# Third and fourth block of a cross-attention kernel: a new order of residual loads, stores, moves, row sums, scores and statistics

## The chip, the cores and the metric

The kernel runs on one core of one Trainium2 chip. The metric is the device time of one execution in microseconds (us). Before the change the median of three runs is 1057.76 us (1057.69 to 1058.13).

The core's engines are named as the profile names them: PE is TensorE's matmul, PEld its weight load, DVE is VectorE, ACT ScalarE, POOL GpSimd, and SP SyncE, which here only issues transfers (DMAs). L949 is line 949 of the kernel before.

## The reference

Sixteen batches of 1024 rows x 512 features are updated by cross-attention to 64 context rows each, with 16 heads of 32 features. Both inputs of the attention are layer-normalised and then scaled and shifted by a per-batch vector.

```python
def _ada_ln(x, c, W_ss, b_ss):
    mu = jnp.mean(x, axis=-1, keepdims=True)
    var = jnp.mean((x - mu) ** 2, axis=-1, keepdims=True)
    h = (x - mu) / jnp.sqrt(var + EPS)
    ss = jax.nn.silu(c) @ W_ss + b_ss
    scale, bias = jnp.split(ss, 2, axis=-1)
    return (1.0 + scale)[:, None, :] * h + bias[:, None, :]
...
xq = _ada_ln(x_q, t_vec, Wss_q, bss_q)
xkv = _ada_ln(x_kv, t_vec, Wss_kv, bss_kv)
q = (xq @ Wq + bq).reshape(B, Lq, nh, dh)
kv = (xkv @ Wkv + bkv).reshape(B, Lkv, 2, nh, dh)
...
scores = jnp.einsum('bqhd,bkhd->bhqk', q, k) / jnp.sqrt(jnp.float32(dh))
attn = jax.nn.softmax(scores, axis=-1)
out = jnp.einsum('bhqk,bkhd->bqhd', attn, v).reshape(B, Lq, H)
return x_q + (out @ Wp + bp)
```

All data are float32.

## The kernel before

The rows are cut into 32 blocks of 512 (two to a batch), numbered 0 to 31. A block passes through these stages; the small functions that do them are called one by one in an order written out by hand: one list of calls for the start (L972 to L1191), a loop over blocks 4 to 29 (L1194 to L1288), and a list for the end. Nothing reorders the calls: each engine runs its instructions in the order in which the calls issue them, and so does SP with its transfers. Waits between engines are put in from the data dependences. In the built program SP's transfers use eight semaphores in turn, so that a transfer is also not issued before the one eight places ahead of it has landed.

The stages of a block i, with their engines and lines:

- `load_x(i)` (SP, L143) loads the block, 1 MB. It needs a free buffer of two, which `turn` of block i-2 gives up. `q_stats(i)` (DVE, L263/L264) takes mean and variance of its 512 rows, in four tiles of 128. `q_scale(i)` computes the inverse root: five small ACT instructions (L279 to L284), then, for blocks above 2, four small POOL instructions (L285 to L288). This is "the root". `hidden(i)` (ACT, L324) normalises in place.
- `turn(i)` (DVE, L503) and `move(i)` (16 small transfers, L516) together transpose the block into `xt`. Block 5 splits the 16 transfers between SP and POOL, block 4 and those from 6 on have all on SP. `scale_features(i)` (ACT, L573) applies scale and shift.
- `feature_sums(i)` (POOL, L608 to L611) and seven `query_product(i, n)` (PE, L633) form the queries with one product fewer than eight, in two PSUM banks, 0 and 1. `query_seed` (ACT, L645) and `query_out` (ACT, L663) copy from them, `query_added` (DVE, L670) adds. Query products 1, 6, 5 and 3 accumulate in bank 0 one after another, so a product has to wait until the copy or add of the one before has read the bank.
- `scores(i, z)` (PE, L681; z is 0 or 1, half of the context rows) writes two tiles of PSUM, each with a maximum taken by DVE (L693) and a copy by ACT (L702). Only two such tiles exist (`ps_s`, tag "s"); scores, mix and, here and there, key and value products take turns in them. `maxima(i)` spreads the maxima (DVE, L715, L724), `subtract(i)` (POOL, L737, two instructions) subtracts them, `weights(i, z)` (ACT, L743) takes the exponential, `total(i)` (POOL, L780) adds the two halves.
- `row_total(i)` (DVE, L785) sums to 128x64 numbers, `inverse_rows(i)` takes their reciprocal (DVE, L800) and sends them to DRAM (`ltd`, SP, L803) and back in another layout (`vr`, SP, four transfers, L805). `spread_rows(i)` (DVE, L811) spreads them.
- `mix(i)` (PE, L841) multiplies weights and values into the two `ps_s` tiles; `divided(i)` (DVE, L821, two halves) divides by the row sums into `ot`.
- `row_sums(i, n)` (POOL, n = 0: L924, L925; n = 1: L928, L929), seven `product(i, n)` (PE, L949) and `added(i, n)` (DVE, L963) do the output projection in PSUM banks 2 and 3, which `biased(i, k)` (ACT, L912) seeds. The result is added to the residual `r`, which `load_residual(i)` (SP, L150, 1 MB) loads. `added(i, 4)` and `added(i, 3)` issue the stores (SP, L965, 512 KB each). There are two `r` buffers, so `load_residual(i)` waits until the stores of block i-2 have landed.
- For every second batch pair, `key_products`, `key_tiles` (DVE, L409), `value_products` and `value_tiles` (DVE, L447) make keys and values.

In the list for the start, block i's scores are computed while the queries of block i+1 and the projections of blocks i-1 and i-2 go on. The change lies in L1094 to L1191: the part from the projection of block 0 to just ahead of the loop. The order in which it puts calls in SP's queue before the change, from 102 us on, is: inverse sums of block 1, move(4), load_x(6), stores of block 0, load_residual(2), inverse sums of block 2, stores of block 1, load_residual(3), load_x(7), SP's half of move(5), inverse sums of block 3, load_x(8), move(6).

Of the kernel before, what the change touches and what calls it, by code (L numbers as in the profile page):

```python
# [20 lines left out]
def cross_attention_block(  # L21
# [118 lines left out]
    def load_x(i):  # L140

        t = xpool.tile([P, NT, H], F32, tag="r" if i == 3 else "x", name=f"x_{i}")
        nc.sync.dma_start(t, rows_of(x, i))  # L143
        x_tiles[i] = t

    def load_residual(i):

        tag = "r" if i < NB - 1 else "x"
        r = xpool.tile([P, NT, H], F32, tag=tag, name=f"r_{i}")
        nc.sync.dma_start(r, rows_of(x, i))  # L150
        r_tiles[i] = r
# [147 lines left out]
    def q_stats(i, ts=range(NT), kvb=None):  # L299

        if ts[0] == 0:
            q_mv[i] = small.tile([P, NT + 1, 2], F32, tag="mvq", name=f"mvq_{i}")
        for t in ts:
            row_stats(q_mv[i][:, t, :], x_tiles[i][:, t, :])
        if kvb is not None:
            row_stats(q_mv[i][:, NT, :], ctx_tiles[kvb])
# [203 lines left out]
    def move(i):  # L510

        ht = ht_tiles.pop(i)
        xt = qpool.tile([P, 4, NC, NT * 32], F32, tag="xt", name=f"xt_{i}")
        for k in range(4):
            for g in range(4):
                (nc.gpsimd if i in (1, 2, 3, 5) and k % 2 else nc.sync).dma_start(  # L516
                    xt[32 * k : 32 * k + 32, g],
                    ht[32 * g : 32 * g + 32, k].rearrange("p c t b -> p c (t b)"),
                )
        xt_tiles[i] = xt  # L520
# [20 lines left out]
    def queries(i, o, later=False):  # L541
        xt, b = xt_tiles[i], i // BPB
        w = wq_tiles.get(b, w_q_sb)
        pq = bank(f"pq_{i}_{o}")
        for c in range(NC):
            nc.tensor.matmul(  # L546
                pq.rearrange("p (g n) -> p g n", g=4),
                lhsT=w[:, c, o * P : (o + 1) * P],
                rhs=xt[:, :, c, :],
                start=(c == 0),  # L550
                stop=(c == NC - 1),
            )
        pq_tiles[i, o] = pq
        if not later:
            queried(i, o)
# [14 lines left out]
    def scale_features(i, cs=range(NC)):  # L570
        xt, b = xt_tiles[i], i // BPB
        for c in cs:
            nc.scalar.activation(  # L573
                xt[:, :, c, :],
                xt[:, :, c, :],
                AF.Identity,
                scale=ss["q"][:, c, b : b + 1],
                bias=ss["q"][:, NC + c, b : b + 1],
            )
# [35 lines left out]
    def query_product(i, n):  # L615

        w, t = sums_of["wq"], sums_of["xt"]
        a, x = {
            1: (query_half(0, 0), feature_half(i, 0, 0)),
            2: (query_half(0, 1), feature_half(i, 1, 0)),  # L620
            3: (w[:, 3], feature_half(i, 1, 1)),
            4: (query_half(1, 1), t[:, 2]),
            5: (w[:, 0], feature_half(i, 0, 1)),
            6: (w[:, 1], t[:, 1]),
            7: (w[:, 2], t[:, 0]),
        }[n]
        k = 0 if n in (1, 6, 5, 3) else 1
        new = n in (1, 7)
        if new:
            qa[k] = bank(f"pq_{i}_{n}", k)  # L630
        for m in range(2):
            for c in range(HC):
                nc.tensor.matmul(  # L633
                    qa[k][:, m * HT : (m + 1) * HT].rearrange("p (g n) -> p g n", g=2),
                    lhsT=a[:, c, m * P : (m + 1) * P],
                    rhs=x[:, :, c, :],
                    start=new and m == 0 and c == 0,
                    stop=c == HC - 1,
                    skip_group_check=True,
                )  # L640
# [33 lines left out]
    def scores(i, z, crossed=False):  # L674

        kt, qt = k_tiles[i // BPB], qt_tiles[i]
        pss = [ps_s.tile([P, 2, TB], F32, tag="s", name=f"ps_{i}_{z}_{e}") for e in range(2)]
        for r in range(HPC):
            rows = slice(32 * r, 32 * r + 32)
            for c in range(NC):  # L680
                nc.tensor.matmul(  # L681
                    pss[r // 2][32 * c : 32 * c + 32, r % 2, :],
                    lhsT=kt[rows, c, z * HK : (z + 1) * HK],
                    rhs=qt[rows, c, :],
                    start=True,
                    stop=True,
                )
        if z == 0:
            m_tiles[i] = small.tile([P, 2, HPC, NJ], F32, tag="m2", name=f"m2_{i}")
        s_sb = big.tile([P, HPC, TB], F32, tag=f"big{i % 2 * 2 + z}", name=f"s_{i}_{z}")  # L690

        def maximum(e):
            nc.vector.tensor_reduce(  # L693
                m_tiles[i][:, z, 2 * e : 2 * e + 2, :],
                pss[e].rearrange("p r (j a) -> p r j a", a=32),
                AX.X,
                ALU.max,
                apply_transpose=True,
            )

        def copied(e):
            nc.scalar.copy(s_sb[:, 2 * e : 2 * e + 2, :], pss[e])  # L702


        for step in (
            ((maximum, 0), (copied, 1), (maximum, 1), (copied, 0))
            if crossed
            else ((maximum, 0), (copied, 0), (maximum, 1), (copied, 1))
        ):
            step[0](step[1])  # L710
        s_tiles[i, z] = s_sb
# [29 lines left out]
    def weights(i, z):  # L741
        p = s_tiles[i, z]
        nc.scalar.activation(p, p, AF.Exp, scale=SCALE)  # L743
# [29 lines left out]
    def total(i):  # L773

        if i == 0:

            t = opool.tile([P, HPC, TB], F32, tag="ot", name="sum_0")
        else:
            t = big.tile([P, HPC, TB], F32, tag=f"big{(i + 1) % 2 * 2}", name=f"sum_{i}")
        nc.gpsimd.tensor_tensor(t, s_tiles[i, 0], s_tiles[i, 1], ALU.add)  # L780
        sum_tiles[i] = t
# [15 lines left out]
    def inverse_rows(i):  # L797

        lt = lt_tiles.pop(i)
        nc.vector.reciprocal(lt, lt)  # L800
        v = small.tile([P, NC, NJ], F32, tag="vr", name=f"vr_{i}")
        d = dram.tile([NC, 32, HPC, NJ], F32, tag="lt", name=f"ltd_{i}")
        nc.sync.dma_start(d.rearrange("c a r j -> (c a) r j"), lt)  # L803
        for r in range(HPC):
            nc.sync.dma_start(v[32 * r : 32 * r + 32], d[:, :, r, :].rearrange("c a j -> a c j"))  # L805
        vt_rows[i] = v
# [112 lines left out]
    def row_sums(i, n):  # L919

        tt = nc.gpsimd.tensor_tensor
        if n == 0:
            s1_tiles[i] = opool.tile([P, HC, HT], F32, tag="s1", name=f"s1_{i}")
            tt(s1_tiles[i], half_rows(i, 1, 0), half_rows(i, 0, 0), ALU.subtract)  # L924
            tt(half_rows(i, 1, 0), half_rows(i, 1, 1), half_rows(i, 1, 0), ALU.subtract)  # L925
        else:
            s2_tiles[i] = opool.tile([P, HC, HT], F32, tag="s2", name=f"s2_{i}")
            tt(s2_tiles[i], half_rows(i, 1, 1), s1_tiles[i], ALU.subtract)  # L928
            tt(half_rows(i, 0, 1), half_rows(i, 0, 1), s2_tiles[i], ALU.subtract)  # L929
# [28 lines left out]
    def added(i, n):  # L958

        m, o = {1: (0, 0), 2: (0, 0), 6: (0, 1), 7: (1, 1), 5: (1, 1), 4: (0, 1), 3: (1, 0)}[n]  # L960
        r = r_tiles[i][:, 2 * m : 2 * m + 2, o * HO : (o + 1) * HO]
        k = 2 if n in (1, 6, 5, 3) else 3
        nc.vector.tensor_add(r, acc[k].rearrange("p (t h) -> p t h", t=2), r)  # L963
        if n in (3, 4):
            nc.sync.dma_start(  # L965
                rows_of(out, i)[:, 2 * m : 2 * m + 2, :], r_tiles[i][:, 2 * m : 2 * m + 2, :]
            )
        if n == 3:
            r_tiles.pop(i)
# [121 lines left out]
    product(0, 5)  # L1091
    added(0, 5)
    turn(4, range(NT))
    move(4)  # L1094
    load_x(6)
    product(0, 4)
    added(0, 4)
    product(0, 3)
    added(0, 3)
    load_residual(2)  # L1100
    weights(2, 0)
    biased(1, 2)
    weights(2, 1)
# [3 lines left out]
    divided(1)  # L1107
    context_hidden(2)
    queries(3, 3)
    q_stats(5)  # L1110
    q_scale(5)
    row_sums(1, 0)
    context_features(2)
    product(1, 1)
    added(1, 1)
# [3 lines left out]
    biased(1, 3)  # L1119
    row_total(2)  # L1120
    inverse_rows(2)


    scale_features(4)
    scores(3, 0, crossed=True)
    feature_sums(4)
    product(1, 7)
    product(1, 6)
# [17 lines left out]
    added(1, 4)  # L1146
    added(1, 3)
    biased(2, 2)
    load_residual(3)
    mix(2)  # L1150
    q_stats(6, (2, 3))
    divided(2)
# [9 lines left out]
    added(2, 1)  # L1162
    product(2, 2)
    added(2, 2)
    weights(3, 1)
    total(3)
    query_product(4, 7)
    query_out(4, 7)
    biased(2, 3)
# [5 lines left out]
    key_tiles(2)  # L1175
    query_product(4, 4)
    query_added(4, 4)
    row_total(3)
    inverse_rows(3)
    scale_features(5)  # L1180
    turn(6, range(NT))
    load_x(8)
# [3 lines left out]
    query_out(4, 3)  # L1186
    feature_sums(5)
    product(2, 7)
    q_stats(7)
    move(6)  # L1190
    q_scale(7)  # L1191

# [196 lines left out]
```

## Time and profile before

| | before |
|---|---|
| median of 3 runs | 1057.76 us |
| the profiled execution | 1058.46 us |
| its span, first to last instruction | 1056.2 us |
| mean granted clock of TensorE | 0.997 |
| PE busy | 1028.8 us (97%) |
| DVE busy | 863.7 us (82%) |
| POOL busy | 762.7 us (72%) |
| PEld busy | 747.5 us (71%) |
| ACT busy | 611.0 us (58%) |

The profile is one execution. Its parts used here are the busy time of each engine in stretches of the span, the chain of work that ended last, and rows of single engines in order of time. A row has the start in us, the busy us, engine, line, operation, output and inputs by the program's names, shapes and count; square brackets hold the idle time of the engine just before and what ended it. A wait for several semaphores is put down to the one that came last, so a releaser can be named that the instruction doesn't read; then the program says what it does wait for. `SPq` rows are the issue of transfers, from the first to the last of a group, and "DMA" pieces of the chain run to their landing.

Some rows around the change: the chain passes move(4) (issued from 106.59 for 10.95 us), load_x(6) (117.64), the stores of block 0 (118.26), load_residual(2) (126.99), and the inverse sums of block 2 (L803 at 127.46, L805 from 132.77). load_residual(3) is issued at 144.58, load_x(7) at 147.18, SP's half of move(5) from 147.92 for 10.03 us, the inverse sums of block 3 at 162.61.

### The profile page before, as it was taken

The numbers are of one execution on the slowest core, as the hardware profiler recorded it, in microseconds if no ns is written. First come the engines' busy times: TensorE is split into PE (matmuls) and PEld (weight loads), VectorE is DVE, ScalarE is ACT, GpSimd is POOL, SyncE is SP. The second block draws the span as 40 slices with busy tenths as digits, with TensorE's granted clock in tenths as the row PEclk, the third lists the DMA queues.
The fourth block names the chain that finished last, engine by engine and source line by source line (L and its number), as shares of the span: only waits on it lengthen the run. The fifth ranks groups of instructions, "written<-read, shape, count | busy, mean of one in ns | idle before, by whom it ended". The sixth has DMA issues, their size and how long they took to land.

```text
span 1056.2 us, 22776 instructions
## 1 busy us (share of the span) xinstructions
PE 1028.8 (97%) x8986; PEld 747.5 (71%) x8986; DVE 863.7 (82%) x1150; ACT 611.0 (58%) x940; POOL 762.7 (72%) x495
## 2 busy tenths in 40 slices
PE   6999889999999999999999999999999999999998
PEld 3635567777777787777777787777777777777433
DVE  5798859987789977988878877898778887776993
ACT  3656645665566655666556666566566765565330
POOL 0479684889768869788668986688886886787340
PEclk9999989999999999999999999999999999999999
DMA  9851554344544444554335544345444443334202
GB/s 333 249 174 41 162 159 125 121 150 148 162 119 137 139 127 143 170 163 127 119 107 162 154 157 135 100 142 155 140 153 147 139 133 115 101 113 161 82 31 90
DMA packets 101562, 147.50 MB, mean 140 GB/s; under 512 B 32040, under 2 KB 32192, under 8 KB 101456
## 3 DMA queue, kind: packets, MB, share of 16 engines
q1 hardware_dynamic: 100432, 143.95, 43.7%
q0 software_dynamic: 1024, 2.10, 0.8%
q8 instruction: 71, 1.16, 0.5%
q14 instruction: 35, 0.29, 0.1%
HBM read 78.95 MB, written 34.54 MB: 107 GB/s over the span
## 4 chain that ended last, share of the span: by engine, by line
PE 86%; DVE 7%; DMA 2%; issue 1%; ACT 1%; POOL 1%; SPq 0%; DVEq 0%; POOLq 0%
PE pp L949 31%; PE pq L633 30%; PE po L841 6%; PE ps L681 6%; PE pq L546 4%; PE pp L868 3%; PE pk L398 3%; PE pv L434 2%; DVE m L693 1%; DVE bs L263 1%; DVE s L737 1%; DMA out_dram<-r 1%; DMA ltd<-lt 1%; DVE lt L785 1%; POOL s L737 1%
## 5 line engine op out<-in xcount | busy, mean ns | idle before, releaser
L737 POOL TENSOR_TENSOR s<-s,mb 128x2048 f32<-128x2048 f32 x58 | 263.2, 4563 | 162.9 <-DVE mb L724 158.9
L702 ACT COPY s<-ps 128x1024 f32<-128x1024 f32 x128 | 129.3, 1012 | 111.7 <-DVE m L693 73.4
L693 DVE TRANSPOSE_TENSOR_REDUCE m<-ps 128x32 f32<-128x1024 f32 x128 | 150.8, 1215 | 30.7 <-PE ps L681 26.9
L949 PE MATMUL pp<-w_p_sb,ot 128*128 128x256 f32 x696 | 162.5, 384 | 4.5 <-ACT workq L284 4.5
L663 ACT ACTIVATE qt<-pq,bias_t 128x256 f32<-128x256 f32 x216 | 89.3, 464 | 115.4 <-PE pq L633 115.2
L963 DVE TENSOR_TENSOR r<-pp,r 128x512 f32<-128x512 f32 x203 | 131.6, 670 | 26.9 <-PE pp L949 19.4
L949 PEld LDWEIGHTS pp<-w_p_sb,ot 128*128 128x128 f32 x696 | 134.0, 193 | 24.4 <-ACT workq L284 4.9
L743 ACT ACTIVATE s<-s 128x2048 f32<-128x2048 f32 x64 | 122.3, 1911 | 44.0 <-POOL s L737 32.6
L780 POOL TENSOR_TENSOR sum<-s,s 128x2048 f32<-128x2048 f32 x29 | 131.7, 4543 | 3.5 <-ACT s L743 3.5
L949 PEld LDWEIGHTS pp<-WT,s 128*128 128x128 f32 x464 | 83.7, 189 | 54.9 <-issue 29.8
L949 PE MATMUL pp<-WT,s 128*128 128x256 f32 x464 | 115.2, 391 | 0.0
L949 PE MATMUL pp<-WT,ot 128*128 128x256 f32 x464 | 109.8, 379 | 3.2 <-POOL ot L925 3.2
L633 PE MATMUL pq<-xt_sums,wq_sums 128*128 128x256 f32 x432 | 104.9, 386 | 0.0
L633 PE MATMUL pq<-xt,wq_sums 128*128 128x256 f32 x432 | 102.8, 381 | 0.0
L633 PEld LDWEIGHTS pq<-xt_sums,wq_sums 128*128 128x128 f32 x432 | 79.8, 190 | 32.2 <-issue 22.4
L633 PE MATMUL pq<-xt,w_q_sb 128*128 128x256 f32 x432 | 102.3, 379 | 0.2 <-ACT pq L645 0.2
L949 PEld LDWEIGHTS pp<-WT,ot 128*128 128x128 f32 x464 | 88.0, 190 | 16.9 <-POOL ot L925 4.1
L324 ACT ACTIVATE x<-x,rstdq 128x512 f32<-128x512 f32 x128 | 96.6, 807 | 1.9 <-DVE rstdq L294 1.9
L670 DVE TENSOR_TENSOR qt<-pq,qt 128x256 f32<-128x256 f32 x108 | 40.6, 417 | 69.7 <-PE pq L633 69.2
L633 PEld LDWEIGHTS pq<-xt,w_q_sb 128*128 128x128 f32 x432 | 81.9, 190 | 12.5 <-issue 0.8
L263 DVE BATCH_NORM_STATS2 bs<-x 128x6 f32<-128x512 f32 x128 | 86.8, 679 | 2.7 <-DMA x<-in_x_dram 2.7
L633 PEld LDWEIGHTS pq<-xt,wq_sums 128*128 128x128 f32 x432 | 80.5, 190 | 11.5 <-issue 1.4
(135 smaller groups left out, 1663.4 us busy)
## 6 DMA issues: line engine op xcount, KB each, us to landing
x<-in_x_dram SPq DMA_DIRECT2D x32, 1024.0 KB, 6.2
r<-in_x_dram SPq DMA_DIRECT2D x32, 1024.0 KB, 5.5
xt<-ht SPq DMA_DIRECT2D x464, 64.0 KB, 2.0
out_dram<-r SPq DMA_DIRECT2D x58, 512.0 KB, 3.7
out_dram<-r SPq DMA_DIRECT2D x12, 256.0 KB, 2.0
wss_q<-in_L_xcond_Wss_q_dram SPq DMA_DIRECT2D x2, 1024.0 KB, 9.1
ctx<-in_ctx_dram SPq DMA_DIRECT2D x8, 256.0 KB, 3.2
wss_kv<-in_L_xcond_Wss_kv_dram SPq DMA_DIRECT2D x2, 1024.0 KB
```

The lines of the kernel that those rows point to most:

```text
L263: nc.vector.bn_stats(bs, r)
L324: nc.scalar.activation(dst, src, AF.Identity, bias=rstd[:, 1, j : j + 1], scale=rstd[:, 0, j : j + 1])
L633: nc.tensor.matmul(qa[k][:, m * HT : (m + 1) * HT].rearrange("p (g n) -> p g n", g=2), lhsT=a[:, c, m * P : (m + 1) * P], rhs=x[:, :, c, : ...
L663: nc.scalar.activation(dst, src, AF.Identity, bias=bq_t[:, o : o + 1])
L681: nc.tensor.matmul(pss[r // 2][32 * c : 32 * c + 32, r % 2, :], lhsT=kt[rows, c, z * HK : (z + 1) * HK], rhs=qt[rows, c, :], start=True, s ...
L693: nc.vector.tensor_reduce(m_tiles[i][:, z, 2 * e : 2 * e + 2, :], pss[e].rearrange("p r (j a) -> p r j a", a=32), AX.X, ALU.max, apply_tra ...
L702: nc.scalar.copy(s_sb[:, 2 * e : 2 * e + 2, :], pss[e])
L737: eng.tensor_tensor(s_tiles[i, z], s_tiles[i, z], mb_tiles[i], ALU.subtract)
L743: nc.scalar.activation(p, p, AF.Exp, scale=SCALE)
L780: nc.gpsimd.tensor_tensor(t, s_tiles[i, 0], s_tiles[i, 1], ALU.add)
L949: nc.tensor.matmul(acc[k][:, t * HO : (t + 1) * HO], lhsT=rows[:, c, t * P : (t + 1) * P], rhs=cols[:, c, :], start=n == 2 and t == 0 and ...
L963: nc.vector.tensor_add(r, acc[k].rearrange("p (t h) -> p t h", t=2), r)
```

## The change

Calls change their places in the list; no function changes, and no work is added or taken away. In the order of the list:

- Block 0's last two products with their stores now come ahead of `move(4)` and `load_x(6)`.
- `load_residual(2)` goes from behind block 0's stores to behind `inverse_rows(2)`, and `load_residual(3)` from ahead of `mix(2)` to behind block 2's second product; on SP this puts it behind load_x(7) and move(5).
- `row_sums(1, 0)` comes ahead of the root of block 5 on POOL.
- `scores(3, 0)` comes ahead of `scale_features(4)`: on ACT the two copies come ahead of the four scalings.
- `q_stats(7)`, `row_total(3)` and `inverse_rows(3)` move up on DVE, from behind the last query products of block 4 to behind block 2's second product. The order on PE is what it was.

```diff
     product(0, 5)
     added(0, 5)
     turn(4, range(NT))
-    move(4)
-    load_x(6)
     product(0, 4)
     added(0, 4)
     product(0, 3)
     added(0, 3)
-    load_residual(2)
+    move(4)
+    load_x(6)
     weights(2, 0)
...
     queries(3, 3)
+    row_sums(1, 0)
     q_stats(5)
     q_scale(5)
-    row_sums(1, 0)
     context_features(2)
...
     row_total(2)
     inverse_rows(2)
-
-
+    load_residual(2)
+
+
+    scores(3, 0, crossed=True)
     scale_features(4)
-    scores(3, 0, crossed=True)
     feature_sums(4)
...
     biased(2, 2)
-    load_residual(3)
     mix(2)
...
     product(2, 2)
     added(2, 2)
+    load_residual(3)
+    q_stats(7)
     weights(3, 1)
     total(3)
+    row_total(3)
+    inverse_rows(3)
     query_product(4, 7)
     query_out(4, 7)
     biased(2, 3)
...
     query_added(4, 4)
-    row_total(3)
-    inverse_rows(3)
     scale_features(5)
     turn(6, range(NT))
...
     product(2, 7)
-    q_stats(7)
     move(6)
     q_scale(7)
```

## The prediction

> **What bounds the kernel now.** I read three views in this order: the busy time by stretch, to find where TensorE is not full; the chain of waits there; and the rows of each engine, to simulate the new order by hand. First the busy time by stretch (columns: length, then busy us and instructions of PE, PEld, DVE, ACT, POOL, then granted clock, DMA share, GB/s).
>
> ```profile
> 100.00:120.00 20.00, 16.92 (x151) 10.51 (x149) 18.98 (x26) 11.43 (x22) 15.19 (x9) 1.00 0.30 62
> 120.00:140.00 20.00, 18.49 (x160) 13.01 (x160) 12.64 (x15) 10.38 (x15) 16.66 (x9) 1.00 0.50 157
> 140.00:160.00 20.00, 16.23 (x112) 14.15 (x116) 10.79 (x20) 10.17 (x17) 14.35 (x17) 0.83 0.68 211
> 160.00:180.00 20.00, 18.87 (x222) 14.60 (x215) 18.58 (x26) 12.16 (x22) 6.66 (x9) 1.00 0.46 107
> 180.00:1030.00 850.00, 847.78 (x7487) 639.07 (x7486) 717.44 (x929) 510.33 (x780) 657.07 (x398) 1.00 0.43 133
> ```
>
> From 180 us on PE is busy 847.8 of 850 us: there the kernel is TensorE's, and the change touches nothing in that loop. What can be won lies between 116 and 173 us, where PE stands idle 3.22 + 0.37 + 0.24 + 4.52 + 1.13 = 9.5 us, and where the clock is below 1. The two large gaps in PE's rows:
>
> ```profile
> 120.14 1.99 PE L949 MATMUL pp<-WT,ot 128*128 128x256 f32 x8 [3.22 <-POOL ot L925]
> ...
> 143.77 6.46 PE L949 MATMUL pp<-w_p_sb,ot 128*128 128x256 f32 x16 [4.52 <-ACT workq L284]
> ```
>
> The second is twice a loss: its 16 matmuls take 6.46 us, where the same 16 took 3.62 us at 112.23. The releaser named (ACT L284) isn't what this product reads: it reads `ot` of block 2, whose first half the division L821 (from 142.42) finishes at 143.6. The chain of waits shows what made that late:
>
> ```profile
> 118.83 8.08 DMA out_dram<-r
> 126.99 0.38 SPq L150
> 127.46 5.29 DMA ltd<-lt
> ...
> 134.09 1.61 DMA vr<-ltd
> 135.72 0.05 DVEq L811
> 135.82 2.31 DVE vb L811
> ```
>
> The inverse sums of block 2 were ready on DVE at 119.53, but their transfer (L803) was issued at 127.46: SP was held by the residual load L150, which waits for block 0's stores to land. DVE's spread then waited 4.56 us. Last, DVE's own row of idle time, which the moved statistics are to fill:
>
> ```profile
> 157.36 0.75 DVE L670 TENSOR_TENSOR qt<-pq,qt 128x256 f32<-128x256 f32 x2 [6.41 <-PE pq L633]
> ```
>
> **What the Trainium skill says.** "TensorE: Matmul & The Clock Gate", Part 1: after an idle window of about 3.4 us, free-running, PE goes to half clock until it has been busy for such a window. The trace agrees: after 3.22 us of idleness the clock stayed 1.00; after 4.52 us it reads 0.50 in 144 to 148 and 0.83 in 148 to 152, and the 16 matmuls cost 2.8 us more. "DMA: Bandwidth & Descriptors", Rules for kernel authors: a transfer that reads what another wrote has to wait for its semaphore. So it is here: L805 is issued 5.3 us after L803. Same page, Issuing engines are not separate DMA queues: all transfers share 16 engines. The trace agrees: ltd took 5.3 us beside a 1 MB load, 1.5 us (102.54 to 104.02) alone. The first page, Architectural detail, also calls ACT and DVE strict FIFO, which I use for each new wait; the rows of this trace come in program order.
>
> **The change part by part.** All times are those of the profiled execution.
>
> *Stores before move(4).* Stores of block 0 need DVE's adds, done at 106.2 and 106.85, so move(4) starts at 107.4 instead of 106.59 and, at its old 10.95 us, ends at 118.35; +0.8 us. The landing of the stores (3.2 us for the pair at 140.32) lies under the move's issue. load_x(6) is issued at 118.4. Cost nothing: xt_4 lands by 120.4, and ACT uses it after that (below).
>
> *load_residual(2) behind the inverse sums' transfers.* L803 goes at 119.65, one microsecond behind the start of load_x(6). An x load takes 6.2 us in the median; before, ltd landed just when the 1 MB load ahead of it did (126.99 + 5.6). So ltd lands at about 124.6; four L805 take 1.75, and vr is there 1.3 us after the last: 128.0 instead of 135.7. r_2 is issued at 126.6, lands at 132.3, and is first used at 141.
>
> *row_sums(1,0) before the root.* POOL's L924/L925 run at 114.0 to 116.65, not 117.47 to 120.09. But product(1,7) also needs the bias copy L912 on ACT, done at 119.35. So PE starts at 119.4: 0.74 of the 3.22 us is won, and the wait goes from POOL to ACT.
>
> *scores(3,0) before scale_features(4).* ACT's two copies run 119.35 to 121.66 (before: 122.28 to 124.2), the four scalings 121.7 to 124.6 (before: to 122.38). scores(3,1) starts behind product(1,6) at 122.85 instead of 124.23. feature_sums(4) on POOL gets its input 2 us later and ends at 129.9; the maxima are spread at 128.7 (before 130.68), so subtract(3) runs 129.9 to 138.9 instead of 130.82 to 139.85: 0.9 us better.
>
> Then PE is 1.8 us ahead (query_product(4,2) at 127.8, before 129.60) and reaches the end of query_product(4,6) at 137.4. DVE: L811 at 129.4 with vr already there; two statistics, two adds, two statistics: before these took 135.82 to 142.42, 6.6 us, now 6.85 as an add waits for PE; divided(2) starts at 136.25, its first half is done at 137.4. The 4.52 us gap goes, and with it the half clock (2.8 us). PE at query_product(4,7): 141.0 instead of 150.23, **9.2 us ahead**.
>
> *q_stats(7), row_total(3) and inverse_rows(3) moved up, load_residual(3) down.* turn(5) ends on DVE at 141.05, and SP issues load_x(7) at 141.15, the residual load no longer ahead of it. In DVE's queue q_stats(7) now stands behind added(2,2) (142.4) and waits for that load. Behind it on DVE: row_total(3), query_added(4,5), key_tiles(2), query_added(4,4), turn(6), value_tiles(2); for query_added(4,5) waits PE (query_product(4,3) writes the same bank), for value_tiles(2) the second half of scores(4,0). **The unknown is this landing.** Bounds: 6.2 us (median of all x loads) and 10.2 (x_7 before, with r_3 ahead of it). I take 7.5, which x_8 took with one move behind it, as x_7 has now: 148.7. SP's half of move(5) and POOL's are issued by 149 and land by 153; POOL's sum of block 3 ends at 151.4, before DVE wants it (152.0). From X = 148.7 by DVE's rows: statistics 3.27, row_total and reciprocal 2.9, query_added 0.8: done at 155.7. PE is ready for query_product(4,3) at 141.0 + 12.3 = 153.3 and waits 2.4 us, short of the 3.22 that left the clock alone. Then 0.7 + 0.8 + 2.5 + 0.7: value_tiles at 160.4, the second half of scores(4,0) runs at 160.4 to 161.0, product(2,6) and query_product(5,1) end at 164.6. The maxima now follow at once (no statistics and root ahead of them), ACT's copies end at 163.1, so scores(4,1) starts at 164.6 instead of 172.19. **Gain 7.6 us**: 9.2 + 1.13 (the old last gap) - 2.4 - 0.35 (wait for value_tiles).
>
> Afterwards SP's load_x(8) and move(6) come 6.2 us earlier only; xt_6 landed at about 182 and was used at 186.36, so 3 us of cover are left. load_residual(3) delays L803 of block 3 to nothing: vr_3 at about 161, used at about 171.
>
> The profiled execution took 1058.46 us (span 1056.2, 2.3 around it), the median run 1057.76. Less 7.6: 1050.9 and **1050.2**.
>
> **The rivals.**
> 1. *Full recovery*: x_7 lands in 6 us or less, so that DVE is never late: 9.2 + 1.13 = 10.3 us, 1047.4. For it: the load starts on idle DMA engines. Against: POOL's and SP's moves come 0.5 us behind it, on the same engines.
> 2. *The gap returns at q_stats(7)*: with 10.2 us PE's wait is 2.4 + 2.7 = 5.1 us, and the half clock comes too: 7.6 - 2.7 - 2.8 = 2.1 us, 1055.6. For it: x_7 did take that long. Against: a megabyte less in its way.
> 3. *The transfers don't come early*: load_x(6) or the store delays ltd so that vr is no earlier than 135.7. Then turn(5) stays at 147.2, and only the 1.13 us gap goes: 1056.6. vr has 1.4 us of slack at 129.4; each microsecond past it costs one, up to 6.3.
> 4. *Slower*: the same place as 2, q_stats(7) held by x_7 on an in-order DVE. The loss grows microsecond by microsecond with X, plus 2.8 for the clock: break-even at X = 153.5 (12.4 us after issue), and 15.5 us would give 1060.9. Before, q_stats(7) ran at 165.88 with x_7 long there. Against: after the first 60 us no x load took over 10.2.
>
> **How the numbers follow.** Forecast (gain 5.5 to 9.2; 1048.5 to 1052.3) 0.63; rival 1 0.13, rival 2 0.12, rival 3 0.08, rival 4 0.04. The range runs from rival 1 to just short of rival 2, 1047.4 to 1055.0, and leaves out half of 2, and 3 and 4: 0.18. About 0.2% (2.1 us) is what a measurement of this kernel can tell from no change. Faster by over 0.2%: 0.63 + 0.13 + 0.08 of rival 2 = 0.84; within: 0.12; slower: 0.04.
>
> **What would show it.** L803 of block 2 issued at about 119.7 and ltd landed by 125; L811 without an idle time before it; PE's gap at 139 gone and the clock at 1.00 throughout 140 to 152; PE's first gap at 2.5 us, ended by ACT L912; a new DVE wait for x before L263 of about 6 us, and a new PE gap of some 2 us before query_product(4,3). Wrong would be: clock under 1 in 150 to 160 (rival 2), or L811 still waiting for vr (rival 3).

## The result, and the profile after

The changed kernel takes 1049.58 us (median of 4 runs, 1047.6 to 1050.43) against 1057.72 us before (4 runs): a ratio of 0.9937, with a 95% interval of 0.9919 to 0.9955. That is 0.63% or some 6.7 us faster by the ratio of the runs, 8.1 us by the medians. The forecast was 1050.2 us in a range of 1047.4 to 1055.0.

The profiled execution took 1047.6 us, span 1045.5 us. It is the fastest of the four, so I don't compare whole spans. In it PE reaches the third part of block 3's queries, where nothing has changed yet, at 95.82 us; before it did at 97.17. Every comparison of traces below is therefore a **distance**, from the start of these eight matmuls (queries(3,2), L546) to the start of scores(4,1) (L681, the last place where PE waited before): 172.19 - 97.17 = 75.02 us before, 162.14 - 95.82 = 66.32 us after. The trace thus gained **8.70 us** where the prediction had 7.6.

The busy time by stretch of the kernel after (length, then busy us and instructions of PE, PEld, DVE, ACT, POOL, then granted clock, DMA share, GB/s):

```profile
100.00:120.00 20.00, 17.63 (x156) 11.56 (x155) 19.13 (x27) 11.72 (x22) 16.38 (x11) 1.00 0.43 116
120.00:140.00 20.00, 19.63 (x170) 14.37 (x169) 18.57 (x26) 14.73 (x24) 16.35 (x12) 1.00 0.43 156
140.00:160.00 20.00, 19.23 (x239) 15.87 (x238) 13.31 (x25) 10.68 (x21) 17.16 (x17) 1.00 0.70 188
160.00:180.00 20.00, 20.00 (x173) 15.20 (x172) 17.54 (x22) 13.32 (x18) 11.61 (x8) 1.00 0.62 188
180.00:1020.00 840.00, 837.77 (x7387) 631.28 (x7387) 709.11 (x916) 503.13 (x772) 646.53 (x395) 1.00 0.42 132
```

The clock is 1.00 in all of them, PE is idle for 3.5 us between 100 and 160, and full from 160 on, as in the loop. PE's rows after, the four that had or got a wait:

```profile
117.94 1.97 PE L949 MATMUL pp<-WT,ot 128*128 128x256 f32 x8 [2.37 <-ACT pp L912]
...
136.24 3.69 PE L949 MATMUL pp<-w_p_sb,ot 128*128 128x256 f32 x16
...
153.08 1.99 PE L633 MATMUL pq<-xt,wq_sums 128*128 128x256 f32 x8 [0.77 <-DVE qt L670]
...
156.73 1.83 PE L681 MATMUL ps<-qt,kt 32*32 32x512 f32 x32
```

The first gap is 2.37 us and is now ended by ACT's bias copy L912. The second (4.52 us) is gone, and product(2,1) with product(2,2) take 3.69 instead of 6.46 us. A new gap of 0.77 us stands ahead of query_product(4,3), and scores(4,0) takes 0.7 us longer than the 1.14 of other scores, as it waits inside. SP's issues after:

```profile
117.61 0.52 SPq L143 DMA_DIRECT2D x<-in_x_dram  x1
118.23 0.48 SPq L803 DMA_DIRECT2D ltd<-lt  x1
123.42 2.71 SPq L805 DMA_DIRECT2D vr<-ltd  x4
126.18 0.43 SPq L150 DMA_DIRECT2D r<-in_x_dram  x1
...
139.65 0.38 SPq L143 DMA_DIRECT2D x<-in_x_dram  x1
```

The inverse sums of block 2 go out at 118.23, half a microsecond behind load_x(6), and land 5.2 us later. On DVE they now come in time, and the wait that the change put in is the one for x_7:

```profile
128.31 2.29 DVE L811 STREAM_TRANSPOSE vb<-vr 128x2048 f32<-128x2048 f32 x1
...
146.05 0.69 DVE L263 BATCH_NORM_STATS2 bs<-x 128x6 f32<-128x512 f32 x1 [5.05 <-DMA x<-in_x_dram]
...
149.52 2.31 DVE L785 TRANSPOSE_TENSOR_REDUCE lt<-sum 128x64 f32<-128x2048 f32 x1 [0.18 <-POOL sum L780]
```

### The profile page after: what moved, and what is told of

Same layout as the page of the kernel before. It is cut to its first block, busy times and chain, and to the rows that moved or that the text cites. A ratio compares the mean times of both kernels' runs of the same rounds, so it can differ in the third digit from the quotient of the medians.

```text
span 1045.5 us, 22774 instructions
## 1 busy us (share of the span) xinstructions
PE 1024.9 (98%) x8986; PEld 744.5 (71%) x8986; DVE 863.4 (83%) x1150; ACT 611.0 (58%) x940; POOL 762.1 (73%) x495
## 4 chain that ended last, share of the span: by engine, by line
PE 88%; DVE 4%; POOL 4%; issue 2%; ACT 1%; SPq 1%; DMA 1%; DVEq 0%; POOLq 0%
PE pp L949 32%; PE pq L633 30%; PE po L841 6%; PE ps L681 6%; PE pq L546 5%; PE pp L868 3%; PE pv L434 2%; PE pk L398 2%; POOL s L737 1%; DVE m L693 1%; SPq L516 1%; POOL sum L780 1%; DVE s L737 1%; DVE mb L724 1%; DMA x<-in_x_dram 0%
## 5 line engine op out<-in xcount | busy, mean ns | idle before, releaser
L702 ACT COPY s<-ps 128x1024 f32<-128x1024 f32 x128 | 129.5, 1013 | 111.0 <-DVE m L693 71.7
L949 PE MATMUL pp<-w_p_sb,ot 128*128 128x256 f32 x696 | 159.8, 379 | 0.0
```

The source lines that it names most:

```text
L949: nc.tensor.matmul(acc[k][:, t * HO : (t + 1) * HO], lhsT=rows[:, c, t * P : (t + 1) * P], rhs=cols[:, c, :], start=n == 2 and t == 0 and ...
```

## The experiments

My theory was that the gain comes from SP: the inverse sums no longer stand behind the residual load that waits for stores, so the idle time at product(2,1) and the half clock behind it go. The rivals: that the new order on ACT, POOL and DVE carries it; that only one of the two SP edits counts; and, for what remained to be gained, that x_7's landing sets the end. Each kernel's times stand against runs of the kernel before on the same chip. Their median was 1055.75 to 1056.42 us beside e1 to e12, so the ratios count and not the medians alone. A distance is read from one profiled execution.

| kernel | median us | ratio to before, 95% | distance us |
|---|---|---|---|
| before | 1057.72 | | 75.02 |
| after | 1049.58 | 0.9937 [0.9919, 0.9955] | 66.32 |
| e1 load_residual(2) alone | 1050.96 | 0.9944 [0.9929, 0.9959] | 68.42 |
| e2 stores first alone | 1052.66 | 0.9963 [0.9948, 0.9977] | 68.58 |
| e10 both of these | 1051.35 | 0.9958 [0.9944, 0.9972] | 68.57 |
| e3 the rest without them | 1055.73 | 0.9995 [0.9985, 1.0005] | 75.91 |
| e12 after, load_residual(2) ahead | 1047.93 | 0.9926 [0.9912, 0.994] | 66.64 |
| e4 after, statistics back | 1050.43 | 0.9946 [0.9928, 0.9964] | 67.77 |
| e5 after, load_residual(3) back | 1052.12 | 0.9965 [0.9953, 0.9978] | 70.72 |
| e6 after, load_x(7) behind move(5) | 1053.37 | 0.9974 [0.9965, 0.9983] | 72.02 |
| e11 before, gap filled | 1056.88 | 1.0005 [0.9995, 1.0015] | 75.71 |
| e7 after, bias copy first | 1048.8 | 0.9929 [0.9917, 0.9941] | 67.54 |
| e8 after, other order on DVE | 1048.05 | 0.9922 [0.9905, 0.9938] | 66.64 |
| e9 e7 and e8 together | 1045.22 | 0.9895 [0.9882, 0.9909] | 63.62 |

### SP's queue: either edit alone, both, and the rest without them

e1, an edit of the kernel before:

```diff
-    load_residual(2)
...
     inverse_rows(2)
+    load_residual(2)
```

> Before, with one edit: load_residual(2) behind inverse_rows(2), the stores still behind move(4) and load_x(6). Measure: from the start of queries(3,2) on PE to the start of scores(4,1), 75.0 us before and 66.3 after. If the held-up transfer of the inverse sums is the cause, this edit alone takes away the 4.5 us idle time at product(2,1) and the half clock behind it (2.8): 67.7 us, some 7.3 us faster than before. If the whole needs the reordering on ACT, POOL and DVE as well, the distance stays above 72 us.

e2, another edit of the kernel before:

```diff
-    move(4)
-    load_x(6)
     product(0, 4)
     added(0, 4)
     product(0, 3)
     added(0, 3)
+    move(4)
+    load_x(6)
     load_residual(2)
```

> Before, with one edit: block 0's stores ahead of move(4) and load_x(6); load_residual(2) still ahead of the inverse sums' transfers. If it was the wait for the stores that held SP, the wait is over by 111 us and this edit alone is nearly as good as the other: the inverse sums are issued at 119.7, land behind two loads of 1 MB at about 128, are spread at 131.5; 68 us from queries(3,2) to scores(4,1), 7 us faster than before. If the residual load has to be behind the inverse sums whatever the stores do, L811 on DVE still waits 2 us or more and the distance is above 70 us.

e10 makes both edits of the kernel before and nothing else.

> Before, with both edits of SP's queue (stores ahead of move(4) and load_x(6); load_residual(2) behind the inverse sums) and none of the rest. The gap at product(2,1) is gone as with either edit alone: 66.8 us from queries(3,2) to scores(4,1) without and 68.5 with one window of half clock at the 3.2 us gap that stays at product(1,7); so the two do not add, and the rest of the change is worth 1 to 2 us over this. If they add, under 66.

e3 is the change without these two: stores, move(4), load_x(6) and load_residual(2) stand as before.

> After, with the stores back behind move(4) and load_x(6) and load_residual(2) back ahead of the inverse sums: what is left is the row sums, the scores ahead of the scalings, the statistics and load_residual(3). By the prediction's third rival only the last gap of 1.1 us goes: 73.9 us from queries(3,2) to scores(4,1), 1.1 us faster than before, half clock still there. If these reorderings carry the gain by themselves: under 70 us.

SP's rows of e1, then of e2:

```profile
117.65 1.00 SPq L965 DMA_DIRECT2D out_dram<-r  x2
119.47 0.34 SPq L803 DMA_DIRECT2D ltd<-lt  x1
126.20 2.53 SPq L805 DMA_DIRECT2D vr<-ltd  x4
128.84 0.39 SPq L150 DMA_DIRECT2D r<-in_x_dram  x1
```

```profile
105.48 1.32 SPq L965 DMA_DIRECT2D out_dram<-r  x2
...
118.53 0.53 SPq L150 DMA_DIRECT2D r<-in_x_dram  x1
119.16 0.45 SPq L803 DMA_DIRECT2D ltd<-lt  x1
126.43 2.62 SPq L805 DMA_DIRECT2D vr<-ltd  x4
```

In both the inverse sums are issued at once (119.47, 119.16) and take 6.7 and 7.3 us behind two megabytes of other traffic; in e10, with one megabyte ahead, 5.4 us. All three are in time: DVE's L811 starts without idle time at 131.96, 131.31 and 131.75, PE's gap at product(2,1) is gone in all, and the distances are 68.4 to 68.6 us. So the edits don't add: each alone takes away 6.4 to 6.6 us of the change's 8.7. Without the old gap and its half clock (4.52 + 2.84 us) the distance before would be 67.7 us; all three lie 0.8 to 0.9 above that. For e10 I had expected 66.8 us when no half clock shows, and it took 68.57 with the clock at 1.00. Rows of PE in e10, and then one of ACT, say why:

```profile
119.66 1.99 PE L949 MATMUL pp<-WT,ot 128*128 128x256 f32 x8 [3.15 <-POOL ot L925]
124.80 1.47 PE L681 MATMUL ps<-qt,kt 32*32 32x512 f32 x32 [1.42 <-ACT s L702]
```

```profile
120.01 2.93 ACT L573 ACTIVATE xt<-xt,ss_q 128x512 f32<-128x512 f32 x4 [1.14 <-DMA xt<-ht]
```

The data of move(4) come later, since move(4) now follows the stores; ACT's scalings wait 1.14 us for them, and the copies that scores(3,1) needs stand behind the scalings. scores(3,1) begins 28.05 us from queries(3,2). In the kernel before it began at 27.06; its row, and then two of e1:

```profile
124.23 1.47 PE L681 MATMUL ps<-qt,kt 32*32 32x512 f32 x32 [0.37 <-ACT s L702]
```

```profile
120.05 3.51 PE L949 MATMUL pp<-WT,ot 128*128 128x256 f32 x8 [3.18 <-POOL ot L925]
...
125.22 1.14 PE L681 MATMUL ps<-qt,kt 32*32 32x512 f32 x32
```

In e1 ACT is not late, but PE ran at half clock behind the gap (3.51 us instead of 1.99), and scores(3,1) began at 28.10. So both lost 1.0 us there, for different reasons. In the whole change the copies come ahead of the scalings, so the later move(4) holds up nothing: the reordering on ACT is what makes the stores' move free.

In the times the three gain less than in the traces: 5.9, 3.9 and 4.4 us by the ratios, where I had expected some 7 of e1 and e2. Their intervals overlap, so the three can't be told apart.

e3 is the counter-test. Without the SP edits nothing is gained: 75.91 us, and no time that can be told from before. Its rows on PE and on DVE:

```profile
142.43 5.09 PE L949 MATMUL pp<-w_p_sb,ot 128*128 128x256 f32 x16 [5.23 <-ACT workq L284]
162.28 3.68 PE L633 MATMUL pq<-xt,wq_sums 128*128 128x256 f32 x8 [2.37 <-DVE qt L670]
```

```profile
155.53 0.69 DVE L263 BATCH_NORM_STATS2 bs<-x 128x6 f32<-128x512 f32 x1 [7.29 <-DMA x<-in_x_dram]
```

The old gap stays, and the statistics wait 7.29 us for x_7, which adds a gap of 2.37 us with half clock. The prediction's third rival gave this case 1.1 us of gain; it missed that the new wait on DVE comes in it too. The reordering on the engines pays only on top of the SP edits: after against e10 it is worth 2.2 us in the traces, while the intervals of the times overlap. It lets scores(3,1) begin at 25.75 us after and at 25.89 in e3, against 28.05 in e10; in e3 the wait for the inverse sums takes this lead away. Whether the row sums' new place or the copies' brings it wasn't tried apart.

e12 undoes the place of load_residual(2) in the change, and leaves the stores first:

```diff
     load_x(6)
+    load_residual(2)
...
     inverse_rows(2)
-    load_residual(2)
```

> After, with load_residual(2) back ahead of the inverse sums' transfers, but with the stores still first, so it doesn't wait. The inverse sums then land behind two loads; vr arrives some 3 us later than after, 1.5 us too late for DVE, which comes to L811 earlier than in the experiment with the stores alone: L811 waits 1 to 2 us and the distance from queries(3,2) to scores(4,1) is 67.5 to 68.5 us. If it was only the wait for the stores that mattered, 66.3.

It took 66.64 us, 0.3 more than after, where I had expected 1.2 to 2.2 more. Its row of DVE:

```profile
129.32 2.31 DVE L811 STREAM_TRANSPOSE vb<-vr 128x2048 f32<-128x2048 f32 x1 [0.44 <-DMA vr<-ltd]
```

The transfers were issued faster than I had reckoned (four L805 in 1.75 us, as against 2.62 in e2), so vr was only 0.44 us late. What had to go was SP's wait for the stores. With the stores first, the place of the residual load is worth 0.3 us in the trace, and in the times nothing that can be told.

### The wait for x_7

e4 puts the statistics back:

```diff
-    q_stats(7)
...
     product(2, 7)
+    q_stats(7)
```

> After, with q_stats(7) back behind product(2,7) on DVE. The 3.3 us of statistics then stand between value_tiles(2) and the root of block 7 that ACT does ahead of the copies of scores(4,0): scores(4,1) about 1.5 us later than after, 67.8 us from queries(3,2). If the move of the statistics is worth nothing (DVE has time for them there), 66.3 us; if the wait for x_7 on DVE costs more than the move brings, less than 66.3.

67.77 us, as expected: the root of block 7 ends on ACT only just ahead of the copies (L284 at 163.22, L702 at 163.31), and PE waits 1.35 us for them. Moving the statistics up is worth 1.45 us, though DVE then waits for x_7. The two kernels' times can't be told apart.

e5 puts load_residual(3) back ahead of mix(2), so that it precedes load_x(7) on SP:

```diff
+    load_residual(3)
     mix(2)
...
     added(2, 2)
-    load_residual(3)
```

> After, with load_residual(3) back ahead of mix(2), so ahead of load_x(7) on SP. If the load that q_stats(7) waits for is slowed by a megabyte ahead of it, x_7 lands some 10 us after issue (6.3 after), L263 on DVE starts 3.8 us later than after, and PE's gap at query_product(4,3) goes from 0.8 to some 4.5 us: 70 us from queries(3,2) to scores(4,1) (66.3 after), 73 with a half clock; 4 to 6 us slower than after. If x_7 has room anyway, 66.3.

e6 lets load_x(7) itself come late:

```diff
     turn(5, range(NT))
-    load_x(7)
     q_scale(6)
     row_sums(2, 0)
     move(5)
+    load_x(7)
```

> After, with load_x(7) behind move(5) on SP. The prediction's slower case: x_7 is issued some 5 us later, q_stats(7) holds DVE in order, and row_total(3), query_added(4,5), key_tiles(2) and value_tiles(2) with it. One us of PE for each us of x_7, and the half clock[...]: 71 to 74 us from queries(3,2) to scores(4,1), 5 to 8 us slower than after. If DVE has slack that the sum has overlooked, under 69.

PE's row at query_product(4,3) in e5, then in e6:

```profile
153.57 3.78 PE L633 MATMUL pq<-xt,wq_sums 128*128 128x256 f32 x8 [2.68 <-DVE qt L670]
```

```profile
156.47 3.78 PE L633 MATMUL pq<-xt,wq_sums 128*128 128x256 f32 x8 [4.86 <-DVE qt L670]
```

In e5 x_7 lands 8.6 us after its issue (6.3 after, 10.2 before, and some 10 expected), so the statistics start 2.25 us later than after, in e6 4.60 us later (both measured from queries(3,2)). PE's gap grows from 0.77 to 2.68 and 4.86 us: 1.91 and 4.09, nearly one for one. The eight matmuls behind it take 3.78 instead of 1.99 us in both: the half clock, also after the gap of only 2.68. Distances 70.72 and 72.02 us. The new wait is the change's weak point, and load_residual(3) out of x_7's way is worth 4.4 us of distance, half clock included. By the ratios e5 is some 3 us slower than after (the intervals just overlap) and e6 some 4 (they are apart), less than I had expected of either.

### The half clock by itself

e11 fills PE's gap in the kernel before with matmuls that nobody reads:

```diff
     query_out(4, 6)
+    junk = bank("junk", 3)
+    for _ in range(6):
+        nc.tensor.matmul(
+            junk, lhsT=w_q_sb[:, 0, :P], rhs=w_q_sb[:, 0, :], start=True, stop=True
+        )
```

> Before, with six matmuls that nobody reads (128x512, about 0.46 us each) put into PE's 4.5 us gap ahead of product(2,1). The order of everything else stays. They run from the adds of block 1 (140.3) to about 143.1[...]. If the 6.46 us of product(2,1) and product(2,2) come from the half clock that follows the idle time, these take 3.7 us and the distance from queries(3,2) to scores(4,1) falls from 75.0 to 72.2 us, 2.8 us faster than before though PE does more. If the two products are slow for another reason (operands, DMA traffic), the distance stays at 75.

```profile
141.44 5.42 PE L1163 MATMUL junk<-w_q_sb 128*128 128x512 f32 x12 [0.72 <-DVE r L963]
146.69 3.62 PE L949 MATMUL pp<-w_p_sb,ot 128*128 128x256 f32 x16
```

I had misread the profile's count: each 128x512 matmul is two instructions of 0.45 us, so the filler took 5.42 us, not 2.8, and ran past the point where product(2,1) could have begun. Product(2,1) and product(2,2) took 3.62 us, against 6.46 in the kernel before. The stretches in which they ran, before and then in e11 (the last three columns are clock, DMA share and GB/s):

```profile
144.00:148.00 4.00, 4.00 (x10) 3.19 (x11) 3.54 (x6) 4.00 (x4) 3.60 (x6) 0.50 0.49 153
148.00:152.00 4.00, 4.00 (x17) 3.38 (x17) 1.00 (x2) 0.01 (x2) 3.98 (x8) 0.83 0.95 315
```

```profile
144.00:148.00 4.00, 4.00 (x14) 2.29 (x13) 4.00 (x6) 3.97 (x8) 2.91 (x6) 1.00 0.54 130
148.00:152.00 4.00, 4.00 (x21) 3.54 (x20) 1.63 (x3) 1.10 (x1) 3.85 (x8) 1.00 1.00 346
```

The traffic is much the same and so are the operands, but the clock is 1.00: the slowness was the clock's. The distance (75.71) doesn't show the 2.8 us saved, for two reasons. The inverse sums landed later (6.4 us after issue instead of 5.3), and the division of block 2 with them, by 1.7 us; and by an estimate from the rows the filler held product(2,1) for 1.8 us more. The time can't be told from before, with 5.4 us more work on PE.

### What was still to be had

e8 changes the order on DVE and SP behind the statistics:

```diff
-    row_total(3)
-    inverse_rows(3)
...
     query_added(4, 4)
+    row_total(3)
+    inverse_rows(3)
     scale_features(5)
-    turn(6, range(NT))
-    load_x(8)
     value_products(2, spare("pv_2"))
     value_tiles(2)
+    turn(6, range(NT))
+    load_x(8)
```

> After, with row_total(3) and inverse_rows(3) behind query_added(4,4) and value_tiles(2) ahead of turn(6) on DVE; q_stats(7) stays up. PE's gap of 0.8 us at query_product(4,3) and the 0.7 us inside scores(4,0) should both go, since what they wait for no longer stands behind the sum of block 3 and the turn: 64.9 us from queries(3,2) to scores(4,1), 1.4 us faster than after. If x_7 itself is the limit, one of the two stays and the distance is 66.

e7 puts the bias copy ahead of the context's features on ACT:

```diff
-    context_features(2)
     product(1, 1)
     added(1, 1)
     product(1, 2)
     added(1, 2)
+    biased(1, 3)
+    context_features(2)
     row_sums(1, 1)
-    biased(1, 3)
```

> After, with biased(1,3) ahead of context_features(2) on ACT (and the four turns of context_features(2) behind product(1,2) on PE). If the bias copy is what product(1,7) waits for, as the prediction has it, PE's gap there goes from 2.4 us to under 0.6, and with it the window of half clock that some executions show there; copies and scores(3,1) move less, as the eight instructions of context_features(2) now stand ahead of the copies: 65.3 to 66.3 us from queries(3,2) to scores(4,1) (66.3 after). If the row sums on POOL are still what comes last, nothing changes.

e9 does both.

> After, with the two edits together: row_total(3) behind query_added(4,4), value_tiles(2) ahead of turn(6), and biased(1,3) ahead of context_features(2). 64 to 65 us from queries(3,2) to scores(4,1), the clock at 1.00 throughout, and 1.5 to 3 us faster than after; if the bias edit only shifts the wait to the copies, the same as with the DVE edit alone, 65.0.

In e8 both waits behind the statistics are gone, but in the profiled execution the gap at product(1,7) is followed by half clock. Its row, and the clock around it:

```profile
119.71 3.58 PE L949 MATMUL pp<-WT,ot 128*128 128x256 f32 x8 [2.52 <-ACT pp L912]
```

```profile
120.00:124.00 4.00, 4.00 (x13) 3.24 (x13) 2.65 (x3) 3.61 (x6) 0.41 (x1) 0.63 0.92 270
```

That product takes 3.58 instead of 1.97 us; less these 1.6 us the distance is 65.0, as expected. In the times e8 can't be told from after. In the kernel after, the gap at the same place (2.37) left the clock alone in the profiled execution, but three of its four runs show a mean clock of 0.998 or 0.999, and only the fastest 1.000; where they lost it no trace shows.

In e7 the gap at product(1,7) falls to 0.55 us, still ended by L912, as the prediction's reading of it says. The gain is lost further on, in these rows of DVE and of PE:

```profile
149.36 2.31 DVE L785 TRANSPOSE_TENSOR_REDUCE lt<-sum 128x64 f32<-128x2048 f32 x1 [2.01 <-POOL sum L780]
```

```profile
152.92 2.58 PE L633 MATMUL pq<-xt,wq_sums 128*128 128x256 f32 x8 [2.01 <-DVE qt L670]
```

PE and DVE come 1.1 us earlier to product(2,1), POOL does not, and with row_total(3) ahead of query_added(4,5) DVE now waits for POOL's sum; in this execution the half clock followed. 67.54 us, outside what I expected, and a time that can't be told from after. With e8's order the sum stands in nobody's way, and so e9 gains more than both apart:

```profile
115.78 1.97 PE L949 MATMUL pp<-WT,ot 128*128 128x256 f32 x8 [0.36 <-POOL rstdq L287]
...
134.83 3.69 PE L949 MATMUL pp<-w_p_sb,ot 128*128 128x256 f32 x16
...
154.48 1.22 PE L681 MATMUL ps<-qt,kt 32*32 32x512 f32 x32
```

(L287 is named for the first, but product(1,7) reads no root; ACT's copy L912 ends at 115.63, just ahead of it.) e9 takes 63.62 us of distance, a little under the 64 to 65 expected, and 1045.22 us (1044.78 to 1045.68), a ratio of 0.9895 to before, against 0.9937 for the change: the intervals are apart. Its four runs lie within 0.9 us, at clocks of 0.999 to 1.000.

## Why the prediction was right

Point by point, with the prediction's times moved by the 1.35 us that the profiled execution after runs early:

- **The inverse sums** were to be issued at 119.65 and land at 124.6: 119.58 and 124.7. That L811 no longer waits held, and so did the landing of ltd together with the load ahead of it.
- **product(1,7)** was to start at 119.4 behind the bias copy: 119.29, and ACT L912 is the releaser named. The row sums' place ahead of the root thus bought 0.85 us of its 3.22, and e7 shows the rest was ACT's.
- **product(2,1)** was to start at 137.5: 137.59. The idle time of 4.52 us and the half clock (6.46 to 3.69 us) went together. At query_product(4,7) PE was 8.95 us ahead, where the prediction had 9.2. The cause is shown by e1, e2 and e10 against e3; that the slow products were the clock's doing by e11.
- **The landing of x_7**, the unknown, was mis-sized: 7.5 us taken, 6.3 to 6.4 measured. So the statistics started 1.3 us earlier than reckoned, the gap at query_product(4,3) was 0.77 and not 2.4 us, and the gain 8.7 and not 7.6. The mechanism and its slope held (e5, e6). The lower bound given, 6.2, was the right one: with half a megabyte of moves from each of SP and POOL behind it, x_7 took 6.3 us, where the median of the x loads after is 5.8.
- **The last gap** of 1.13 us went, as said, and e4 shows that it was the place of the statistics. scores(4,0), with its wait inside, took 0.61 us more than before (1.83 and 1.22), where the prediction had 0.35. Together: 8.95 + 1.13 - 0.77 - 0.61 = 8.70 us, the distance gained.

Two arguments failed, though the time came out. The first: the prediction counted the stores' move only as a cost, of nothing, and gave the whole earlier transfer to load_residual(2). The two are each other's substitute (e1, e2, e10), and with the stores first, moving the residual load is worth 0.3 us (e12). The second: that a gap of 2.4 us is safe because 3.22 us had left the clock alone. At the same place, product(1,7), half clock came after gaps of 3.18 (e1), 3.15 (e2), 3.02 (e11) and 2.52 us (e8), and not after 3.22 (before), 3.15 (e10), 2.59 (e6) or 2.37 (after); elsewhere it came after 2.68 (e5), 2.37 (e3) and 2.01 us (e7). A single execution doesn't give a threshold, and that the clock stayed at 1.00 in the profiled execution after, as forecast, was in part luck. By their mean clocks the other runs probably hold such a window: the distance gained 8.7 us, the runs' medians 8.1.

## What to carry to other kernels

On a queue that only issues transfers, look at what each entry waits for before asking how long it takes: a load that waits for a buffer holds back the small transfer behind it, and it is enough that either the wait is over sooner or the small one stands ahead. When work is moved up into an engine's idle time, check that the data it needs are there too, and order what stands behind it by who waits for it. And a gap on TensorE costs more than its length now and then: e9, in which the gaps of 2.37 and 0.77 us are down to 0.36 and none, has its four runs within 0.9 us, the change its four within 2.8.

## What was not expected of the hardware

- The Trainium skill ("TensorE: Matmul & The Clock Gate", Part 1) says that half clock follows an idle window of about 3.4 us, and that the window is free-running. The runs agree in that the length of a gap alone doesn't decide: at product(1,7) one of 3.15 us brought half clock in e2 and not in e10. They differ in the length: gaps of 2.0 to 2.7 us, shorter than such a window, were enough in e3, e5, e7 and e8. In e4 it even came after a gap of 1.35 us, next to scores of 32 rows; the clock there:

```profile
164.00:168.00 4.00, 2.73 (x36) 1.44 (x37) 3.67 (x5) 1.76 (x4) 0.35 (x2) 0.86 0.55 120
168.00:172.00 4.00, 4.00 (x15) 3.34 (x14) 2.69 (x4) 3.88 (x5) 0.00 (x0) 0.72 0.35 84
```

  These short gaps all stand next to matmuls that are listed with a tile of 32*32 (scores) or 128*32 (value products, L434). How much such matmuls count as activity wasn't tried, and stays open.
- 32 KB of inverse sums took 1.5 us to land with the DMA engines idle, 4.7 to 6.4 us behind one load of 1 MB (e8, e11; 5.2 after), and 7.3 us behind two (e2). Before and after, they landed within 0.3 us of the load issued ahead of them.
- What a stretch of half clock costs depends on the waits around it: at product(1,7) all of its 1.6 us in e8, but 1.0 of its 1.5 us in e1, as PE no longer had to wait for ACT's copies behind it.
